# A four-layer graph network: neighbour rows of layers 2 and 3 summed by VectorE into a pair of sums in PSUM, in place of TensorE products with the identity

## The chip, the cores and the metric

The kernel runs on one core of a Trainium2 chip. The metric is the device time of one execution in microseconds (us), as the median of several runs. TensorE is PE (its weight loads PEld), VectorE is DVE, ScalarE is ACT, GpSimd is POOL, SyncE is SP.

## The reference

Four graph layers, each behind a layer norm, a ReLU and a residual, over 6250 nodes of 256 features and 106,250 edges (100,000 random ones and a loop per node). Layer 0 is attention with 8 heads of 32, layer 1 a gated recurrent update, layer 2 a relational layer with 8 edge types, layer 3 a graph attention with a batch norm. The two that the change touches, cut to their core:

```python
# layer 2: h = relu(layernorm(x))
hW = einsum('nd,rde->rne', h, weight)
m = segment_sum(hW[edge_type, src], dst)
x = x + h @ sl_w.T + sl_b + m / maximum(deg, 1)
...
# layer 3: loops added to the edges
xh = (x @ W).reshape(N, H, D)
e = leaky_relu(a_src[src] + a_dst[dst], 0.2)
alpha = softmax of e over the edges of each dst
out = segment_sum(xh[src] * alpha, dst) + bias
return batchnorm(out) + x
```

Both are sums over the neighbours of a node: plain in layer 2, weighted per head in layer 3. All values are float32.

## The kernel before

The nodes are sorted by the number of their edges and cut into 49 blocks of 128 (one node per partition). Every block has a number of slots, `CAPS`, one neighbour of each of its 128 nodes per slot: 39, 25, 24, 23, and so on down to 9, in all 822. A prefix builds these lists on the chip.

Each layer is a stage ("f0" to "f3") with a loop over the 49 blocks. A stage gathers the 822 slots with one indirect DMA each, issued by POOL: 128 rows of 1 KB, one to each partition (in layer 3 rows of 264 floats, the last 8 the heads' attention terms). `Slots.fill` takes a tile `v` for a chunk of up to 8 slots and issues its gathers (L1129). A `v` tile comes from a pool with a fixed number of buffers (8 in layer 2, 7 in layer 3); when all are in use POOL waits until the last reader of the oldest is done. Stages f0 and f1 have an order written by hand; in f2 and f3 the tile scheduler lays down the order of each engine's instructions from the loop. Every engine then runs its own list in order and waits on semaphores.

Layer 2 (stage f2), block by block: for every slot PE multiplies the slot's rows by the identity and adds up in PSUM tile `pa` (L1516; a float32 product is two passes). SP loads the block's x into `xb` (L1518). DVE makes xb = pa * (1/degree) + xb (L1519), then the layer norm on DVE and ACT (L514 to L523, ACT L523 the ReLU), transposes on PE (L531) copied by ACT (`ht`, L533), xb + h stored as x of layer 3 (L1523, L1524), the product with layer 3's weights (L540), its copy by ACT into `xa` (L1528), the attention terms on DVE (L1530, L1531) kept in `asd`, and the store of `xa` to DRAM (L1534). `xa` is what layer 3 gathers.

Layer 3 (stage f3), block by block: gathers into `v`; for each chunk, once it has landed, DVE adds attention terms into `s` (L1556); the own row's term (L1560), leaky ReLU (L1561), and in `weights_of` the softmax: mask (L1611), maximum (L1615), subtract (L1616), exp on ACT (L1617), the loop's factor (L1619), sum (L1621), reciprocal (L1622), and the weights into PSUM tile `ps_w` (L1624). SP loads the block's own rows `xh` (L1565). DVE multiplies xh by its weight (L1567) and PE puts it into PSUM tile `pm` (L1569); DVE multiplies each chunk in place by its weights (L1572), PE adds every slot to `pm` (L1574). DVE adds the bias into `o` (L1575), ACT squares it (L1584), PE adds o and its square over the nodes for the batch norm (L1586). In the program's order the L1556 of a later block stands among the work of earlier ones. After the last block come the norm, the residual and 49 scatters of rows to the output (L1123, POOL).

For scale: in f1, DVE already adds up slots, there with both operands in SBUF (L1386 to L1393).

Of the kernel before, what the change touches and what calls it, by code (L numbers as in the profile page):

```python
# [8 lines left out]
F32 = mybir.dt.float32  # L9
BF16 = mybir.dt.bfloat16  # L10
I32 = mybir.dt.int32
AF = mybir.ActivationFunctionType
# [5 lines left out]
P = 128  # L18
# [8 lines left out]
D = 256  # L27
H = 8
DH = 32
# [1118 lines left out]
class Fast(Kernel):  # L1148
# [13 lines left out]
    def ps(self, shape, kind):  # L1162
        return self.psum.tile(shape, F32, name="ps_" + kind, tag="ps_" + kind, bufs=self.bufs[kind])

    def constants(self):
        nc = self.nc
        self.ident = self.c([P, P], F32, "ident")
        make_identity(nc, self.ident)
        self.icol = self.c([P, 1], F32, "icol")
        nc.gpsimd.iota(self.icol, pattern=[[1, 1]], base=0, channel_multiplier=1,  # L1170
                       allow_small_or_imprecise_dtypes=True)
        self.ones = self.c([P, P], F32, "ones")
        nc.vector.memset(self.ones, 1.0)
        self.eps = self.c([P, 1], F32, "eps")
        nc.vector.memset(self.eps, EPS)
# [63 lines left out]
def sparse(ctx: ExitStack, tc: tile.TileContext, K, S, qv_d, h1_d, rel_d, xa_d, rows_d, wc_d, bc_d, b_ih, w_hh,  # L1239
           b_hh, w_rel, w_sl, b_sl, w_gat, att_src, att_dst, b_gat, gamma, beta, out):  # L1240

    nc = tc.nc
# [3 lines left out]
    with K.stage("f0", a=4, w=2, k=2), tc.tile_pool(name="f0", bufs=2) as pool:  # L1246
        heads = lambda x: x.rearrange("p (h d) -> p h d", h=H)
# [107 lines left out]
    rel_idx = K.c([P, NB, J], I32, "rel_idx")  # L1355
    with K.stage("f1", t=2, g=3, m=3), tc.tile_pool(name="f1w", bufs=1) as wp, tc.tile_pool(name="f1", bufs=2) as pool:
# [132 lines left out]
        with tc.manual_schedule(engines={nc.tensor.engine, nc.vector.engine, nc.scalar.engine}):  # L1489
            for k in range(NB + 4):  # L1490
                s, p, g, m, o = (f(order[k - d]) if 0 <= k - d < NB else nothing()
                                 for d, f in enumerate((sums, products, gates, messages, selves)))
# [8 lines left out]


    asd = ctx.enter_context(tc.tile_pool(name="asd", bufs=1)).tile([P, NB, 2, H], F32, name="asd", tag="asd")
    with K.stage("f2", t=2, m=4, a=2), tc.tile_pool(name="f2w", bufs=1) as wp, tc.tile_pool(name="f2", bufs=2) as pool:
        w = K.weights(wp, w_gat, "w_gat")
        att = wp.tile([P, 2, D], F32, name="att", tag="att")
        for k, vec in enumerate((att_src, att_dst)):
            nc.sync.dma_start(att[:, k, :], bass.AP(tensor=vec.tensor, offset=vec.offset,
                                                    ap=[[0, P], [1, D]]))
        for i in range(NB):  # L1510
            nd = CAPS[i]
            pa = K.ps([P, D], "a")
            for c, n in S.chunks(i, 8):
                v = S.fill(pool, "v", 8, rel_d, i, c, n, 8, D, rel_idx)
                for j in range(n):
                    nc.tensor.matmul(pa, K.ident, v[:, j, :], start=c + j == 0, stop=c + j == nd - 1)  # L1516
            xt = pool.tile([P, D], F32, name="xb", tag="xb")
            nc.sync.dma_start(xt, K.block(x2_d, i))  # L1518
            nc.vector.scalar_tensor_tensor(xt, pa, S.rcnt[:, i: i + 1], xt, op0=ALU.mult, op1=ALU.add)  # L1519
            h = K.norm(pool, xt)  # L1520
            ht = K.transposed(pool, h, "ht")

            nc.vector.tensor_add(xt, xt, h)  # L1523
            nc.sync.dma_start(K.block(x3_d, i), xt)  # L1524
            pm = K.ps([P, D], "m")
            K.product(pm, ht, w)
            xa = pool.tile([P, D + H], F32, name="xa", tag="xa")
            nc.scalar.activation(xa[:, :D], pm, AF.Copy)  # L1528
            tmp = pool.tile([P, 2, D], F32, name="tmp", tag="tmp")
            nc.vector.tensor_mul(tmp, att, xa[:, None, :D].to_broadcast([P, 2, D]))  # L1530
            nc.vector.tensor_reduce(asd[:, i], tmp.rearrange("p a (h d) -> p a h d", h=H), axis=AX.X,  # L1531
                                    op=ALU.add)
            nc.scalar.activation(xa[:, D:], asd[:, i, 0, :], AF.Copy)
            nc.sync.dma_start(K.block(xa_d, i), xa)  # L1534


    with K.stage("f3", m=2, a=2, w=2), tc.tile_pool(name="f3w", bufs=1) as wp, tc.tile_pool(name="f3", bufs=2) as pool:
        bias = K.row(wp, b_gat, D, "b_gat")
        gam = K.row(wp, gamma, D, "gamma")
        bet = K.row(wp, beta, D, "beta")  # L1540
        o = wp.tile([P, NB, D], F32, name="o", tag="o")

        twice = wp.tile([P, NB], F32, name="twice", tag="twice")
        nc.vector.tensor_scalar_add(twice, S.own, 1.0)
        x3 = wp.tile([P, NB, D], F32, name="x3", tag="x3")
        sums = [K.ps([P, D], "m") for _ in range(2)]
        first = wp.tile([P, D], F32, name="first", tag="first")
        for i in range(NB):
            n = P if i < NB - 1 else NLAST
            nd = CAPS[i]  # L1550
            nc.sync.dma_start(x3[:, i, :], K.block(x3_d, i))
            s = pool.tile([P, J + 1, H], F32, name="s", tag="s", bufs=3)
            held = []
            for c, m in S.chunks(i, 8):
                v = S.fill(pool, "v", 7, xa_d, i, c, m, 8, D + H, S.idx)
                nc.vector.tensor_add(s[:, c: c + m, :], v[:, :m, D:],  # L1556
                                     asd[:, i, 1, None, :].to_broadcast([P, m, H]))
                held.append((c, m, v))

            nc.vector.tensor_add(s[:, nd, :], asd[:, i, 0, :], asd[:, i, 1, :])  # L1560
            nc.vector.scalar_tensor_tensor(s[:, : nd + 1, :], s[:, : nd + 1, :], NEG_SLOPE,  # L1561
                                           s[:, : nd + 1, :], op0=ALU.mult, op1=ALU.max)
            w = weights_of(K, pool, s, nd, S.mneg[:, i, :nd], 1.0, twice=twice[:, i: i + 1])
            xh = pool.tile([P, D], F32, name="xh", tag="xh")
            nc.sync.dma_start(xh, K.block(xa_d, i)[:, :D])  # L1565
            xv = xh.rearrange("p (h d) -> p h d", h=H)
            nc.vector.tensor_mul(xv, xv, w[:, nd, :, None].to_broadcast([P, H, DH]))  # L1567
            pm = K.ps([P, D], "a")
            nc.tensor.matmul(pm, K.ident, xh, start=True, stop=False)  # L1569
            for c, m, v in held:  # L1570
                vv = v[:, :m, :D].rearrange("p j (h d) -> p j h d", h=H)
                nc.vector.tensor_mul(vv, vv, w[:, c: c + m, :, None].to_broadcast([P, m, H, DH]))  # L1572
                for j in range(m):
                    nc.tensor.matmul(pm, K.ident, v[:, j, :D], start=False, stop=c + j == nd - 1)  # L1574
            nc.vector.tensor_add(o[:, i, :], pm, bias)  # L1575
            if i == 0:

                pf = K.ps([P, D], "a")
                nc.tensor.matmul(pf, K.ones, o[:, 0, :], start=True, stop=True)
                nc.vector.tensor_scalar(first, pf, 1.0 / P, None, op0=ALU.mult)  # L1580
                nc.vector.tensor_sub(o[:, 0, :], o[:, 0, :], first)
                nc.vector.tensor_sub(bias, bias, first)
            sq = pool.tile([P, D], F32, name="sq", tag="sq")
            nc.scalar.activation(sq, o[:, i, :], AF.Square)  # L1584
            for p, x in zip(sums, (o[:n, i, :], sq[:n, :])):
                nc.tensor.matmul(p, K.ones[:n, :], x, start=i == 0, stop=i == NB - 1)  # L1586
        mean, shift, sc = (wp.tile([P, D], F32, name=x, tag=x) for x in ("mean", "shift", "sc"))
        nc.vector.tensor_scalar(mean, sums[0], 1.0 / N, None, op0=ALU.mult)
        nc.vector.tensor_mul(shift, mean, mean)
        nc.vector.scalar_tensor_tensor(sc, sums[1], 1.0 / N, shift, op0=ALU.mult, op1=ALU.subtract)  # L1590
        nc.vector.tensor_scalar_max(sc, sc, 0.0)
        nc.scalar.activation(sc, sc, AF.Sqrt, bias=K.eps)
        nc.vector.reciprocal(sc, sc)
        nc.vector.tensor_mul(sc, sc, gam)
        nc.vector.tensor_mul(mean, mean, sc)
        nc.vector.tensor_sub(shift, bet, mean)
        for b0, m in [(0, 1), (1, 2), (3, 3)] + [(b, min(4, NB - b)) for b in range(6, NB, 4)]:
            ob, xb = o[:, b0: b0 + m, :], x3[:, b0: b0 + m, :]
            nc.vector.tensor_mul(ob, ob, sc[:, None, :].to_broadcast([P, m, D]))
            nc.vector.tensor_add(xb, xb, shift[:, None, :].to_broadcast([P, m, D]))  # L1600
            nc.vector.tensor_add(xb, xb, ob)
            for i in range(b0, b0 + m):
                n = P if i < NB - 1 else NLAST
                S.scatter(out, S.node(i)[:n], x3[:n, i, :], "out")
# [211 lines left out]
```

## Time and profile before

| what | us |
|---|---|
| median of 3 runs | 4894.41 (4892.23 to 4895.73) |
| the profiled execution | 5607.33 |
| its span | 5605.5 |
| gathers of layer 0, first start to last | 368.0 to 1621.8 |
| layer 1 | 1679.0 to 2982.9 |
| layer 2 | 3060.2 to 4251.5 |
| layer 3 | 4287.7 to 5459.4 |
| scatters of the output | 5489.7 to 5589.0 |

The profile is of one execution, which took 713 us longer than the median of the runs; its mean granted TensorE clock is 0.706 of full. A group's row in the profile tells line, engine, operation and tiles, then busy time, mean duration in ns, and the engine's idle time ahead of it with what ended it ("issue": nothing that the profile shows; "remote": a signal whose sender it can't name). A timeline row has start, duration, engine, line and tiles.

POOL's idle time ahead of L1129, by what ended it, over the whole span: PE L1574 70.6 us (25 times), PE L1516 56.4 (26 times), "remote" 191.2 (48 times).

### The profile page before, as it was taken

The numbers are of one execution on the slowest core, as the hardware profiler recorded it, in microseconds if no ns is written. First come the engines' busy times: TensorE is split into PE (matmuls) and PEld (weight loads), VectorE is DVE, ScalarE is ACT, GpSimd is POOL, SyncE is SP. The second block draws the span as 40 slices with busy tenths as digits, with TensorE's granted clock in tenths as the row PEclk, the third lists the DMA queues.
The fourth block names the chain that finished last, engine by engine and source line by source line (L and its number), as shares of the span: only waits on it lengthen the run. The fifth ranks groups of instructions, "written<-read, shape, count | busy, mean of one in ns | idle before, by whom it ended". The sixth has DMA issues, their size and how long they took to land. (4 is left out here: it accounts for less than half of the span.)

```text
span 5605.5 us, 32468 instructions
## 1 busy us (share of the span) xinstructions
PE 2734.4 (49%) x8412; PEld 1806.8 (32%) x8413; DVE 2620.8 (47%) x5034; ACT 858.1 (15%) x1807; POOL 3448.3 (62%) x3546
## 2 busy tenths in 40 slices
PE   5654444444444766665445443433443544555551
PEld 2323323333332333332222232333332333333440
DVE  4437768776774776766665011111111333333343
ACT  2320111111221332322222000000011000000000
POOL 4326666666646665666663666666665666666666
PEclk7876666666666877877767576766776667766775
DMA  4466667676745544454442333333334333333331
GB/s 156 134 202 196 192 204 207 200 211 199 208 146 166 159 148 147 149 156 144 151 139 93 97 104 104 100 104 108 110 114 145 96 99 101 101 101 100 100 100 47
DMA packets 328275, 775.54 MB, mean 138 GB/s; under 512 B 87464, under 2 KB 172324, under 8 KB 321552
## 3 DMA queue, kind: packets, MB, share of 16 engines
q0 software_dynamic: 196864, 595.62, 37.3%
q1 hardware_dynamic: 117358, 163.66, 8.6%
q10 hardware_dynamic: 13858, 14.09, 0.8%
q8 instruction: 70, 1.15, 0.1%
q14 instruction: 125, 1.02, 0.1%
HBM read 637.90 MB, written 135.19 MB: 138 GB/s over the span
## 5 line engine op out<-in xcount | busy, mean ns | idle before, releaser
L1129 POOL DMA_INDIRECT v<-h,rec_in x822 | 848.6, 1032 | 454.3 <-issue 237.1
L1129 POOL DMA_INDIRECT v<-rel,rel_idx x822 | 789.5, 960 | 479.4 <-issue 234.5
L1129 POOL DMA_INDIRECT v<-xa,rec_in x822 | 783.6, 953 | 424.0 <-issue 265.7
L1129 POOL DMA_INDIRECT qv<-qv,rec_in x822 | 783.9, 954 | 412.2 <-issue 380.1
L1300 PE MATMUL ps_a<-qv,ident 128*128 128x256 f32 x1644 | 517.2, 471 | 251.7 <-issue 238.6
L1574 PE MATMUL ps_a<-v,ident 128*128 128x256 f32 x1644 | 473.7, 442 | 129.7 <-issue 122.7
L1300 PEld LDWEIGHTS ps_a<-qv,ident 128*128 128x128 f32 x1644 | 391.6, 242 | 385.0 <-issue 285.6
L1516 PE MATMUL ps_a<-v,ident 128*128 128x256 f32 x1644 | 463.4, 435 | 91.9 <-issue 75.0
L540 PE MATMUL ps_m<-w_rel,h2t 128*128 128x512 f32 x784 | 438.9, 723 | 35.1 <-ACT res L1466 19.0
L1574 PEld LDWEIGHTS ps_a<-v,ident 128*128 128x128 f32 x1644 | 372.8, 228 | 225.6 <-issue 151.2
L1516 PEld LDWEIGHTS ps_a<-v,ident 128*128 128x128 f32 x1644 | 357.5, 222 | 175.1 <-issue 94.9
L1262 DVE TENSOR_TENSOR tmp<-qv,ps_k 128x1280 f32<-128x1280 f32 (+4 forms) x183 | 247.1, 1350 | 215.1 <-DMA qv<-qv,rec_in 130.2
L1295 PE MATMUL ps_a<-row,ident 128*128 128x256 f32 x98 | 58.5, 698 | 486.0 <-issue 244.3
L1530 DVE TENSOR_TENSOR tmp<-att,xa 128x512 f32<-128x512 f32 x49 | 34.0, 693 | 557.2 <-ACT xa L1528 389.6
L540 PEld LDWEIGHTS ps_m<-w_rel,h2t 128*128 128x128 f32 x784 | 182.3, 240 | 260.0 <-issue 224.0
L1263 DVE TENSOR_REDUCE s<-tmp 128x40 f32<-128x1280 f32 (+4 forms) x183 | 247.2, 1351 | 10.0 <-DVE tmp L1262 2.0
L531 PE MATMUL ps_t<-ident,h 128*128 128x128 f32 x196 | 50.6, 347 | 388.1 <-ACT h L523 183.8
L1298 DVE TENSOR_TENSOR qv<-qv,ps_w 128x1280 f32<-128x1280 f32 (+4 forms) x183 | 235.0, 1345 | 0.0
L1519 DVE SCALAR_TENSOR_TENSOR xb<-ps_a,rcnt_in,xb 128x256 f32<-128x256 f32 x49 | 23.7, 484 | 448.4 <-remote 363.6
L1572 DVE TENSOR_TENSOR v<-v,ps_w 128x2048 f32<-128x2048 f32 (+7 forms) x124 | 233.0, 1914 | 0.0
L1409 PE MATMUL ps_t<-ident,total 128*128 128x128 f32 x98 | 31.2, 417 | 399.5 <-DVE total L1403 269.8
L540 PE MATMUL ps_m<-w_gat,ht 128*128 128x256 f32 x196 | 80.4, 552 | 290.5 <-ACT ht L533 191.2
(298 smaller groups left out, 4139.0 us busy)
## 6 DMA issues: line engine op xcount, KB each, us to landing
rel<-res SPq DMA_DIRECT2D x49, 1024.0 KB
rows<-mrow SPq DMA_DIRECT2D x49, 512.0 KB
fx<-xb SPq DMA_DIRECT2D x147, 128.0 KB
qv<-qv,rec_in POOLq DMA_INDIRECT x822
v<-h,rec_in POOLq DMA_INDIRECT x822
v<-rel,rel_idx POOLq DMA_INDIRECT x822
v<-xa,rec_in POOLq DMA_INDIRECT x822
qv<-mrow ACTq DMA_DIRECT2D x49, 256.0 KB
```

The lines of the kernel that those rows point to most:

```text
L531: nc.tensor.transpose(pt[:, k, :], x[:, k * P: (k + 1) * P], self.ident)
L540: self.nc.tensor.matmul(out, xt[:, k, :], w[:, k, :], start=start and k == 0, stop=stop and k == n - 1)
L1129: self.nc.gpsimd.indirect_dma_start(out=out, out_offset=None, in_=table, in_offset=bass.IndirectOffsetOnAxis(ap=idx, axis=0))
L1262: nc.vector.tensor_mul(tmp[:, :n, :], qv[:, :n, :D], pk[:, None, :].to_broadcast([P, n, D]))
L1263: nc.vector.tensor_reduce(s[:, c: c + n, :], tmp[:, :n, :].rearrange("p j (h d) -> p j h d", h=H), axis=AX.X, op=ALU.add)
L1295: nc.tensor.matmul(pm, K.ident, row[:, 2, :], start=True, stop=False)
L1298: nc.vector.tensor_mul(v, v, w[:, c: c + n, :, None].to_broadcast([P, n, H, DH]))
L1300: nc.tensor.matmul(pm, K.ident, qv[:, j, D: 2 * D], start=False, stop=c + j == nd - 1)
L1516: nc.tensor.matmul(pa, K.ident, v[:, j, :], start=c + j == 0, stop=c + j == nd - 1)
L1530: nc.vector.tensor_mul(tmp, att, xa[:, None, :D].to_broadcast([P, 2, D]))
L1572: nc.vector.tensor_mul(vv, vv, w[:, c: c + m, :, None].to_broadcast([P, m, H, DH]))
L1574: nc.tensor.matmul(pm, K.ident, v[:, j, :D], start=False, stop=c + j == nd - 1)
```

## The change

A new helper, `both`, ends a sum: ACT copies the second half of a [128, 2, 256] PSUM tile to SBUF, DVE adds it to the first half. Layer 2's `pa` and layer 3's `pm` become such pairs. In layer 2 ACT copies the first two slots into the pair, and DVE adds the others, two slots (512 elements) at a time, PSUM onto PSUM; the `v` tiles have 10 buffers in place of 8. In layer 3 DVE multiplies the own row straight into the pair's first half and slot 0 into its second; the other slots are multiplied in place as before and added two at a time; the 7 buffers stay. The PE products at L1516, L1569 and L1574 go. The number of PSUM tiles of each kind changes (f2: products 4 to 2, sums 2 to 4; f3: sums 2 to 4), and `sq` has 3 buffers.

Lines after the helper move down by 7, and further on by more: the first copy is L1525, layer 2's adds L1527, `both` L1168 (ACT) and L1169 (DVE), L1556 becomes L1568, L1572 and L1567 become L1579, layer 3's adds are L1592, L1575 becomes L1595.

```diff
@@ -1162,6 +1162,13 @@
     def ps(self, shape, kind):
         return self.psum.tile(shape, F32, name="ps_" + kind, tag="ps_" + kind, bufs=self.bufs[kind])
 
+    def both(self, pool, sums):
+
+        rest = pool.tile([P, D], F32, name="rest", tag="rest")
+        self.nc.scalar.activation(rest, sums[:, 1, :], AF.Copy)
+        self.nc.vector.tensor_add(sums[:, 0, :], sums[:, 0, :], rest)
+        return sums[:, 0, :]
+
     def constants(self):
         nc = self.nc
         self.ident = self.c([P, P], F32, "ident")
@@ -1501,7 +1508,7 @@
 
 
     asd = ctx.enter_context(tc.tile_pool(name="asd", bufs=1)).tile([P, NB, 2, H], F32, name="asd", tag="asd")
-    with K.stage("f2", t=2, m=4, a=2), tc.tile_pool(name="f2w", bufs=1) as wp, tc.tile_pool(name="f2", bufs=2) as pool:
+    with K.stage("f2", t=2, m=2, a=4), tc.tile_pool(name="f2w", bufs=1) as wp, tc.tile_pool(name="f2", bufs=2) as pool:
         w = K.weights(wp, w_gat, "w_gat")
         att = wp.tile([P, 2, D], F32, name="att", tag="att")
         for k, vec in enumerate((att_src, att_dst)):
@@ -1509,11 +1516,16 @@
                                                     ap=[[0, P], [1, D]]))
         for i in range(NB):
             nd = CAPS[i]
-            pa = K.ps([P, D], "a")
+            pa = K.ps([P, 2, D], "a")
             for c, n in S.chunks(i, 8):
-                v = S.fill(pool, "v", 8, rel_d, i, c, n, 8, D, rel_idx)
-                for j in range(n):
-                    nc.tensor.matmul(pa, K.ident, v[:, j, :], start=c + j == 0, stop=c + j == nd - 1)
+                v = S.fill(pool, "v", 10, rel_d, i, c, n, 8, D, rel_idx)
+                for k in range(0, n, 2):
+                    m = min(2, n - k)
+                    if c + k == 0:
+                        nc.scalar.activation(pa, v[:, :2, :], AF.Copy)
+                    else:
+                        nc.vector.tensor_add(pa[:, :m, :], pa[:, :m, :], v[:, k: k + m, :])
+            pa = K.both(pool, pa)
             xt = pool.tile([P, D], F32, name="xb", tag="xb")
             nc.sync.dma_start(xt, K.block(x2_d, i))
             nc.vector.scalar_tensor_tensor(xt, pa, S.rcnt[:, i: i + 1], xt, op0=ALU.mult, op1=ALU.add)
@@ -1534,7 +1546,7 @@
             nc.sync.dma_start(K.block(xa_d, i), xa)
 
 
-    with K.stage("f3", m=2, a=2, w=2), tc.tile_pool(name="f3w", bufs=1) as wp, tc.tile_pool(name="f3", bufs=2) as pool:
+    with K.stage("f3", m=2, a=4, w=2), tc.tile_pool(name="f3w", bufs=1) as wp, tc.tile_pool(name="f3", bufs=2) as pool:
         bias = K.row(wp, b_gat, D, "b_gat")
         gam = K.row(wp, gamma, D, "gamma")
         bet = K.row(wp, beta, D, "beta")
@@ -1563,15 +1575,23 @@
             w = weights_of(K, pool, s, nd, S.mneg[:, i, :nd], 1.0, twice=twice[:, i: i + 1])
             xh = pool.tile([P, D], F32, name="xh", tag="xh")
             nc.sync.dma_start(xh, K.block(xa_d, i)[:, :D])
-            xv = xh.rearrange("p (h d) -> p h d", h=H)
-            nc.vector.tensor_mul(xv, xv, w[:, nd, :, None].to_broadcast([P, H, DH]))
-            pm = K.ps([P, D], "a")
-            nc.tensor.matmul(pm, K.ident, xh, start=True, stop=False)
+            heads = lambda x: x.rearrange("p j (h d) -> p j h d", h=H)
+            times = lambda out, x, j0, j1: nc.vector.tensor_mul(
+                heads(out), heads(x), w[:, j0:j1, :, None].to_broadcast([P, j1 - j0, H, DH]))
+
+            pm = K.ps([P, 2, D], "a")
+            times(pm[:, 0:1, :], xh[:, None, :], nd, nd + 1)
             for c, m, v in held:
-                vv = v[:, :m, :D].rearrange("p j (h d) -> p j h d", h=H)
-                nc.vector.tensor_mul(vv, vv, w[:, c: c + m, :, None].to_broadcast([P, m, H, DH]))
-                for j in range(m):
-                    nc.tensor.matmul(pm, K.ident, v[:, j, :D], start=False, stop=c + j == nd - 1)
+                k = 0
+                if c == 0:
+                    times(pm[:, 1:2, :], v[:, :1, :D], 0, 1)
+                    k = 1
+                times(v[:, k:m, :D], v[:, k:m, :D], c + k, c + m)
+                while k < m:
+                    n2 = min(2, m - k)
+                    nc.vector.tensor_add(pm[:, :n2, :], pm[:, :n2, :], v[:, k: k + n2, :D])
+                    k += n2
+            pm = K.both(pool, pm)
             nc.vector.tensor_add(o[:, i, :], pm, bias)
             if i == 0:
 
@@ -1580,7 +1600,7 @@
                 nc.vector.tensor_scalar(first, pf, 1.0 / P, None, op0=ALU.mult)
                 nc.vector.tensor_sub(o[:, 0, :], o[:, 0, :], first)
                 nc.vector.tensor_sub(bias, bias, first)
-            sq = pool.tile([P, D], F32, name="sq", tag="sq")
+            sq = pool.tile([P, D], F32, name="sq", tag="sq", bufs=3)
             nc.scalar.activation(sq, o[:, i, :], AF.Square)
             for p, x in zip(sums, (o[:n, i, :], sq[:n, :])):
                 nc.tensor.matmul(p, K.ones[:n, :], x, start=i == 0, stop=i == NB - 1)
```

## The prediction

> **What bounds the kernel now.** I read the page's busy shares first, then its costliest groups, then the windows cut at the stages.
>
> ```profile
> PE 2734.4 (49%) x8412; PEld 1806.8 (32%) x8413; DVE 2620.8 (47%) x5034; ACT 858.1 (15%) x1807; POOL 3448.3 (62%) x3546
> ...
> L1129 POOL DMA_INDIRECT v<-rel,rel_idx x822 | 789.5, 960 | 479.4 <-issue 234.5
> L1129 POOL DMA_INDIRECT v<-xa,rec_in x822 | 783.6, 953 | 424.0 <-issue 265.7
> ...
> L1574 PE MATMUL ps_a<-v,ident 128*128 128x256 f32 x1644 | 473.7, 442 | 129.7 <-issue 122.7
> ...
> L1516 PE MATMUL ps_a<-v,ident 128*128 128x256 f32 x1644 | 463.4, 435 | 91.9 <-issue 75.0
> ```
>
> ```profile
> 3060.00:4255.00 1195.00, 526.46 (x1850) 401.18 (x1848) 146.32 (x360) 83.10 (x222) 789.46 (x822) 0.68 0.36 106
> 4255.00:5430.00 1175.00, 566.08 (x1898) 434.01 (x1898) 404.28 (x771) 41.89 (x113) 763.51 (x801) 0.69 0.38 104
> ```
>
> The columns of the windows are length, then PE, PEld, DVE, ACT, POOL, granted clock, DMA share, GB/s. In layers 2 and 3 POOL is the busiest engine by far. Its 0.30 us "issue" after each gather is part of the gather's price, so its pace is start to start. The timeline of layer 2 shows that:
>
> ```profile
> 3599.50 0.95 POOL L1129 DMA_INDIRECT v<-rel,rel_idx  x1 [0.31 <-issue]
> 3600.75 0.95 POOL L1129 DMA_INDIRECT v<-rel,rel_idx  x1 [0.30 <-issue]
> 3602.01 0.95 POOL L1129 DMA_INDIRECT v<-rel,rel_idx  x1 [0.31 <-issue]
> ...
> 3619.05 0.38 ACT L533 ACTIVATE ht<-ps_t 128x256 f32<-128x256 f32 x1 [27.56 <-remote]
> ...
> 3619.97 0.95 POOL L1129 DMA_INDIRECT v<-rel,rel_idx  x1 [5.70 <-remote]
> ```
>
> One gather takes 1.257 us. 822 of them are 1033 us; layer 2's gathers run from 3060.2 to 4251.5 (1191), layer 3's from 4287.7 to 5459.4 (1172). So 158 and 139 us are stalls, which look like PE's fault: POOL waits for a buffer that PE has not freed. The last two rows say otherwise. ACT at 3619.05 waits for transposes whose PE rows ended at 3592.2; for 27 us nothing that PE finished reached anyone, and then everything moved at once. I read that as a burden of the profiled execution. The check is a sum over POOL's path without such stalls: 366.7 (start of layer 0's gathers) + 3288 x 1.257 = 4133 + 49 row gathers 62 + layer 1's longer gathers 822 x (1.032-0.953) = 65 + the gaps between stages 54, 76 and 35 + 29 to the first scatter + 49 scatters 62 = 4883 us. The profiled execution took 5607.33, the median of the runs is 4894.41. The runs thus have about 11 us of POOL stalls left in four layers, where the profile has some 700. I forecast against the median: a removed PE wait is worth nothing much, a new wait counts in full.
>
> **Layer 2.** Gone are 1644 PE passes. They lie beside POOL: PE is busy 526 of 1195 us even in the profile, so their end is worth 0 to 11 us (that remainder); I take 0. New on DVE are 374 adds (L1527) and 49 in `both`, new on ACT 98 copies. No row has DVE with PSUM on both sides. The near rows, 512 elements wide:
>
> ```profile
> L1530 DVE TENSOR_TENSOR tmp<-att,xa 128x512 f32<-128x512 f32 x49 | 34.0, 693 | 557.2 <-ACT xa L1528 389.6 <-issue 167.5
> ...
> L1575 DVE TENSOR_TENSOR o<-ps_a,b_gat 128x256 f32<-128x256 f32 x43 | 18.2, 423 | 360.8 <-remote 216.4 <-PE ps_a L1574 136.3 <-issue 8.0
> ```
>
> L1428, 512 wide with one PSUM operand, takes 684 ns, L1530 wholly in SBUF 693: PSUM shows no surcharge. The Trainium skill speaks against that (Perfetto Trace Analysis, Optimizing Scalar/DVE Operations): DVE pays about 60 ns of access per instruction on SBUF and about 125 on PSUM. By the row an add is 0.69, 0.72 start to start in a chain; by the rule, with 65 ns more, 0.785, so 797 adds are 574 or 626 us. I take the row; the 52 us between them are DVE time, and reach POOL only where DVE is late. In layer 2 DVE goes to 146 + 374 x 0.72 + 49 x 0.43 = 436 us of 1033. In the changed program's order on DVE, the add that frees a chunk stands at least 47 gathers (59 us) from anything it must wait for, thanks to ten buffers. So layer 2 costs 0. ACT's copies (about 0.6 and 0.38 us, from L1528's 383 ns for 256 wide) add 48 us to 83, under the same cover; without it `both` would add 0.8 us to each block's chain, 39 us. That happens once: before layer 3 starts POOL waits for the last block's xa, whose sum now ends with adds, copy and `both` in place of two PE passes: +2 us.
>
> **Layer 3.** PE loses L1569 and L1574, worth 0 again (0 to 11, shared with layer 2). DVE gains 423 adds and 49 in `both`, about 326 us on 404: 730 of 1033. By block: one of 9 slots has about 10 to 11.4 us on DVE against 9 x 1.257 = 11.3 on POOL, one of 16 about 15.5 against 20.1. So DVE doesn't bound, on average. But it runs in order, and now it is the engine that frees chunks. This is DVE's order from one block of 19 slots in the changed program:
>
> ```
> 4783 L1568 TensorTensor s_17287<-v_17298,asd_13287 128x64 [waits DMASW4_49,DMASW5_49,DMASW3_49,DMASW6_49,DMASW2_49,DMASW7_49,DMASW1_49,DMASW0_49]
> 4784 L1592 TensorTensor ps_a_17262<-ps_a_17262,v_17222 128x512 [waits DVE_49]
> 4785 L1568 TensorTensor s_17287<-v_17308,asd_13287 128x24 [waits DMASW3_49,DMASW2_49,DMASW1_49]
> 4786 L1568 TensorTensor s_17353<-v_17354,asd_13287 128x64 [waits DMASW4_49,DMASW5_49,DMASW3_49,DMASW6_49,DMASW2_49,DMASW7_49,DMASW1_49,DMASW0_49]
> 4787 L1592 TensorTensor ps_a_17262<-ps_a_17262,v_17222 128x256 [waits DVE_49]
> ```
>
> Chunk v_17222 is block i's first, v_17354 is block i+2's first, and row 4787 is the last reader of v_17222. L1568 waits until all eight gathers of its chunk have landed. With seven buffers, three of block i, three of i+1 and the first of i+2 fill the pool; the next gather needs v_17222's buffer. So POOL, having issued the eighth gather of v_17354, must wait until that very gather has landed and DVE has done rows 4786 and 4787. Before, PE freed the chunk and didn't stand behind L1556, so the nearest such wait was 9 gathers off. What landing takes, from layer 3's timeline before:
>
> ```profile
> 4931.57 0.95 POOL L1129 DMA_INDIRECT v<-xa,rec_in  x1 [0.30 <-issue]
> ...
> 4934.49 0.23 DVE L1556 TENSOR_TENSOR s<-v,asd 128x64 f32<-128x64 f32 x1 [9.72 <-DMA v<-xa,rec_in]
> ```
>
> From the start of the last gather to DVE's start: 2.92 us (2.8 to 3.2 elsewhere). The skill's fit (DMA: Bandwidth & Descriptors, Anatomy of one DMA — SWDGE (gpsimd) path: 2.0 us plus bytes over 436 GB/s) gives 2.3 for 132 KB; the row decides, as it includes the issue. A place thus costs 2.92 + 0.23 (L1568) + 0.42 (add) + about 0.1 (signals) - 1.257 (the start that would have come anyway) = 2.4 us; by the rule 1.8. Walking the order with seven buffers, it occurs at 14 places: blocks 4 to 6 and 11 to 21, the ones with three chunks where the look-ahead stands so. At four of them another 0.7 us of add lies between. 10 x 2.4 + 4 x 3.2 = 37 us; by the rule 28. Bounds: 0 if the runs' landing is hidden, 60 if it takes 4.5 us as at layer 3's start (5.4 to 5.7 there).
>
> Block 0 (39 slots, five chunks). POOL wants its first chunk back at 4356.86 in the profile. DVE has the weights at 4350.5, and then, in the new order, own row and slot 0 (0.84), the multiplies of chunks 1 to 5 (2.0 + 3 x 2.28 + 2.0) and between them chunk 1's adds (3 x 0.72 + 0.42): 14.3 us, free at 4364.8, so 7.9 us late. Before, chunk 1 was free after its multiply and 16 PE passes of 0.24 us, about 4357.2, in the profile later only by the stall. So +7.5. After the last gather of layer 3, adds and `both` of the last two blocks replace PE work: +3.6 us before the final norm. The third sq buffer and the wider PSUM tiles cost 0.
>
> **Sum.** 0 + 2 + 37 + 7.5 + 3.6 = 50 us; 4894 + 50 = 4944. An add that is 0.1 us dearer brings some 8 us more, landing at 4.5 us 25 more, landing by the rule 9 less: own range 4915 to 4985.
>
> **Rivals.**
> Faster: the stalls are the kernel's, in the runs too, and other things in my sum of 4883 are shorter there. For: POOL's waits are named "PE ps_a". Then PE leaving the path takes, say, half of 297 us, 148 - 50 = 98 net: 4796. Against: the sum leaves only 11 us. It decides in this rival's favour if more than 60 us of PE waits exist in the runs. Chance 0.17, with small gains as likely as large.
> Same: DVE is ahead of my walk, or the waits fall into stalls that are there anyway, or the adds' waits are as before; or the change doesn't do what it says, as PE was never in the way and DVE isn't either. 4894. Chance 0.08.
> Slower by more, at DVE against POOL: in layer 1, where DVE sums slots, gathers take 1032 ns and not 953. If adds in layers 2 and 3 do this, 1644 x 0.079 = 130 us: 5074 with the waits. For it: the one stage with such sums. Against: layer 1's adds read two SBUF operands, the new ones one. Chance 0.05. The main case is itself on the slower side: 0.70.
>
> **Numbers.** Faster 0.17, within 0.2% (10 us, about what a measurement can tell from no change) 0.08, slower 0.75. Range 4875 to 5000: main case with its bounds, same case, and the smallest gains; left out are larger gains (0.14) and the 130 us.
>
> **What will show it.** Right: 14 waits of POOL in layer 3 on DVE L1592, each 2 to 3.5 us, always with L1568 just before; block 0's of 7 to 8; none in layer 2; adds at 0.69 us; gathers at 1.257. In the profiled execution the PE-flush stalls of layers 2 and 3 should shrink, so its own time may fall while the runs rise. Wrong: runs below 4885, or waits by DVE in layer 2, or L1592 above 0.85 us.

## The result, and the profile after

The changed kernel takes 4941.68 us (median of 4 runs, 4939.28 to 4944.01) against 4894.61 of the kernel before (4892.23 to 4895.73): 47.1 us more, a ratio of 1.0097 (95% interval 1.0079 to 1.0114). The forecast was 4944. In the profile of before, and in the jobs (sets of executions measured together) of ten of the twelve kernels below, every execution was stretched: it took some 600 to 700 us more, the kernel before's too, so such numbers are compared only with the kernel before in the same job.

The profiled execution of the changed kernel, with a span of 4938.8 us, is one of the four runs above, so it shows what the runs do. Its page, the rows that answer to those of before:

```profile
PE 1776.5 (36%) x5027; PEld 1050.7 (21%) x5027; DVE 3077.0 (62%) x5978; ACT 918.5 (19%) x1954; POOL 3469.6 (70%) x3546
...
L1129 POOL DMA_INDIRECT v<-rel,rel_idx x822 | 792.0, 963 | 307.7 <-issue 229.4
L1129 POOL DMA_INDIRECT v<-xa,rec_in x822 | 786.6, 957 | 313.8 <-issue 254.5
L1129 POOL DMA_INDIRECT qv<-qv,rec_in x822 | 786.8, 957 | 250.6 <-issue 201.9
L1527 DVE TENSOR_TENSOR ps_a<-ps_a,v 128x512 f32<-128x512 f32 (+1 forms) x374 | 254.7, 681 | 605.6 <-DMA v<-rel,rel_idx 592.9
```

The windows of layers 2 and 3 (columns as before):

```profile
2650.00:3711.00 1061.00, 135.51 (x296) 71.72 (x296) 395.94 (x824) 132.40 (x344) 791.99 (x822) 0.50 0.41 121
3711.00:4795.00 1084.00, 96.62 (x186) 54.41 (x186) 618.85 (x1273) 52.70 (x141) 786.65 (x822) 0.50 0.41 115
```

PE's busy time in the two layers is down to 136 and 97 us, DVE has its work, and POOL is as busy as it was (792 and 787 us). Layer 2's gathers start from 2651.77 to 3692.89 us, 1041 us: 822 at POOL's pace, 1.261 us from start to start in the median, without one longer wait. Layer 3's, from 3711.95 to 4793.37, take 1081. What POOL waited for (total, times, longest; a wait of 0.3 is the ordinary step between gathers):

```profile
POOL v L1129 <- DVE s L1573: 31.5, 11, 3.0
...
POOL v L1129 <- DVE ps_a L1527: 14.0, 46, 0.3
...
POOL v L1129 <- DVE s L1631: 11.0, 3, 3.9
POOL v L1129 <- DVE s L1568: 7.7, 1, 7.7
...
POOL v L1129 <- DVE ps_a L1592: 2.4, 8, 0.3
```

Layer 2's adds (L1527) hold POOL at no place. Layer 3 has 11 + 3 + 1 waits, 45.7 us of the 47.1 when each is counted without its 0.30 us step. Counting layer 3's gathers from zero, the fourteen stand before gathers 163, 184, 205, 303, 322, 340, 358, 376, 394, 412, 429, 446, 463 and 480: the second chunk of blocks 6 to 8 and 13 to 23, two blocks after those that the prediction names, as it said. The single one is at gather 55, block 0's buffer. One of the fourteen in the timeline, before gather 184:

```profile
3952.95 0.96 POOL L1129 DMA_INDIRECT v<-xa,rec_in  x1 [0.30 <-issue]
3956.10 0.22 DVE L1568 TENSOR_TENSOR s<-v,asd 128x64 f32<-128x64 f32 x1 [7.29 <-DMA v<-xa,rec_in]
3956.24 0.42 DVE L1592 TENSOR_TENSOR ps_a<-ps_a,v 128x256 f32<-128x256 f32 x1
3956.58 0.33 DVE L1573 SCALAR_TENSOR_TENSOR s<-s 128x176 f32<-128x176 f32 x1
3956.82 0.69 DVE L1592 TENSOR_TENSOR ps_a<-ps_a,v 128x512 f32<-128x512 f32 x1
3956.94 0.95 POOL L1129 DMA_INDIRECT v<-xa,rec_in  x1 [3.03 <-DVE s L1573]
```

DVE sits idle for 7.29 us until the gather of 3952.95 has landed; only then comes the last add on the old chunk (3956.24), and POOL goes on 0.28 us after that add ends. The releaser named, L1573, is the row that ended nearest to POOL's start; what POOL needed is the add ahead of it, the last reader of the buffer. So read the rows before the restart, not the name alone.

### The profile page after: what moved, and what is told of

It is laid out like the page before. It is cut to its first block, busy times and chain, and to the rows that moved or that the text cites. A ratio compares the mean times of both kernels' runs of the same rounds, so it can differ in the third digit from the quotient of the medians.

```text
span 4938.8 us, 27151 instructions
## 1 busy us (share of the span) xinstructions
PE 1776.5 (36%) x5027; PEld 1050.7 (21%) x5027; DVE 3077.0 (62%) x5978; ACT 918.5 (19%) x1954; POOL 3469.6 (70%) x3546
## 5 line engine op out<-in xcount | busy, mean ns | idle before, releaser
L1527 DVE TENSOR_TENSOR ps_a<-ps_a,v 128x512 f32<-128x512 f32 (+1 forms) x374 | 254.7, 681 | 605.6 <-DMA v<-rel,rel_idx 592.9
L1307 PE MATMUL ps_a<-qv,ident 128*128 128x256 f32 x1644 | 456.4, 446 | 9.1 <-DVE qv L1305 9.0
L1307 PEld LDWEIGHTS ps_a<-qv,ident 128*128 128x128 f32 x1644 | 372.0, 230 | 108.8 <-DVE qv L1305 44.1
L1606 PE MATMUL ps_m<-o,ones 128*128 128x256 f32 (+1 forms) x98 | 59.8, 714 | 898.7 <-DVE o L1595 896.0
L1568 DVE TENSOR_TENSOR s<-v,asd 128x64 f32<-128x64 f32 (+7 forms) x124 | 26.3, 212 | 464.3 <-DMA v<-xa,rec_in 447.6
L1393 DVE TENSOR_TENSOR v<-v 128x512 f32<-128x512 f32 (+2 forms) x211 | 187.5, 889 | 183.9 <-DMA v<-h,rec_in 158.0
L1592 DVE TENSOR_TENSOR ps_a<-ps_a,v 128x512 f32<-128x512 f32 (+1 forms) x423 | 277.1, 655 | 0.4
L531 PEld LDWEIGHTS ps_t<-ident,h 128*128 128x128 f32 x196 | 26.2, 187 | 1086.4 <-ACT h L523 800.0
L1606 PEld LDWEIGHTS ps_m<-o,ones 128*128 128x128 f32 (+1 forms) x98 | 24.5, 311 | 934.0 <-DVE o L1595 930.6
L1579 DVE TENSOR_TENSOR v<-v,ps_w 128x1792 f32<-128x1792 f32 (+7 forms) x124 | 220.4, 1811 | 0.0
L1486 DVE SCALAR_TENSOR_TENSOR xb<-res,ownr,xb 128x256 f32<-128x256 f32 x392 | 190.7, 487 | 10.9
```

Source lines behind the costliest of these rows:

```text
L531: nc.tensor.transpose(pt[:, k, :], x[:, k * P: (k + 1) * P], self.ident)
L1307: nc.tensor.matmul(pm, K.ident, qv[:, j, D: 2 * D], start=False, stop=c + j == nd - 1)
L1393: nc.vector.tensor_add(v[:, :k, :D], v[:, :k, :D], v[:, m - k: m, :D])
L1486: nc.vector.scalar_tensor_tensor(xt, res[:, r, :], S.ownr[:, i, r: r + 1], xt, op0=ALU.mult, op1=ALU.add)
L1527: nc.vector.tensor_add(pa[:, :m, :], pa[:, :m, :], v[:, k: k + m, :])
L1579: times = lambda out, x, j0, j1: nc.vector.tensor_mul(heads(out), heads(x), w[:, j0:j1, :, None].to_broadcast([P, j1 - j0, H, DH]))
```

## The experiments

The expectations weigh these readings of the 47 us. Theory A: POOL waits for chunk buffers in layer 3, because of where DVE's adds stand in its order. Theory B: the adds cost by their number or price, wherever they stand. Theory C: layer 2 gains by PE's absence, and layer 3 loses more than the whole shows. Theory D (in e3): in source order DVE has too little room. Edits are cut to their core; a minus stands for the changed kernel, in e6 for the kernel before.

**Layer 2 alone** (e1, and e10 in another job): the changed kernel with all lines of layer 3's stage as before, at their core

```diff
-                    nc.vector.tensor_add(pm[:, :n2, :], pm[:, :n2, :], v[:, k: k + n2, :D])
+                    nc.tensor.matmul(pm, K.ident, v[:, j, :D], start=False, stop=c + j == nd - 1)
```

> Layer 2 as in the change (DVE adds, ten buffers), layer 3 as before. Theory A (POOL's pace sets the time, the loss sits in layer 3's chunk buffers): no POOL wait in layer 2, about 2 us more at the step from layer 2 to 3, so 4896 to 4898 us against 4894.6, ratio 1.0005. Theory B (DVE adds in PSUM cost wherever they stand): 374 of the 797 adds, so 47 x 374/797 = 22 us, 4917. Theory C (layer 2 gains by PE's absence and layer 3 loses more than the whole shows): below 4885.

> Layer 2 as in the change, layer 3 as before, in the hope of a job that runs the kernel before at about 4895 us. Theory A: no POOL wait in layers 2 and 3, the time within 5 us of before's (4890 to 4899), as PE's sums were never what POOL waited for. Theory C (PE's sums did hold POOL up somewhere, and layer 3's waits hid that in the whole): below 4885.

Measured: 5492.07 against 5533.10 in the first job, ratio 0.9926 (0.9896 to 0.9957); 5546.36 against 5581.08 in the second, 0.9940 (0.9921 to 0.9959). Both jobs were stretched, so the absolute times expected do not apply. There, layer 2 gains: its gathers took 1124.0 and 1126.6 us, where those of the kernel before took 1169.9 in the profile of another stretched job (e12) and 1191.3 on the page of before. This is what theory C expected, though only in these executions: in the result's own profile layer 2's gathers are at POOL's pace, and the kernel before has little room for such a gain in its runs, as the account below says. The row of layer 2 in e10's windows:

```profile
3052.00:4180.00 1128.00, 124.26 (x270) 65.86 (x270) 382.32 (x777) 122.72 (x319) 855.68 (x822) 0.50 0.39 112
```

POOL is busy 856 us with the same 822 gathers that took 792 in the result's profile; its own gathers are drawn out.

**Layer 3 alone** (e2): the changed kernel with all lines of layer 2's stage as before.

```diff
-                v = S.fill(pool, "v", 10, rel_d, i, c, n, 8, D, rel_idx)
+                v = S.fill(pool, "v", 8, rel_d, i, c, n, 8, D, rel_idx)
...
-                        nc.vector.tensor_add(pa[:, :m, :], pa[:, :m, :], v[:, k: k + m, :])
+                    nc.tensor.matmul(pa, K.ident, v[:, j, :], start=c + j == 0, stop=c + j == nd - 1)
```

> Layer 3 as in the change, layer 2 as before. Theory A: the same 14 waits in layer 3, about 40 us, and block 0's, so 4894.6 + 45 = 4940 us (4935 to 4945), ratio 1.009. Theory B: 423 of 797 adds, 25 us, 4920. Theory C: above 4950.

Measured: 5541.00 against 5533.10, ratio 1.0021 (1.0006 to 1.0037): slower, by some 12 us at the ratio and not 45. In a stretched execution POOL stands still for some 130 to 150 us in each of layers 2 and 3 anyway; that a new wait falls partly into that is likely, not shown. The sign fits A; the size tells nothing apart.

**Layer 3's DVE in source order** (e3, e7, e9; e5 with layer 2 as before). Same instructions on DVE, same seven buffers; only the order is fixed:

```diff
-        for i in range(NB):
+        with tc.manual_schedule(engines={nc.vector.engine}):
+            for i in range(NB):
```

> The changed kernel, with layer 3's DVE instructions held in the order of the source: a block's multiplies and adds all stand before the next block's first s<-v. Same instructions, same seven buffers. Theory A: the add that frees a chunk no longer stands behind the wait for the chunk two blocks on, so the 14 waits and block 0's go: 4941.7 - 45 = 4897 us (4892 to 4902). Theory B (the adds themselves, their number or price in PSUM, are the cost): 4940, no change. Theory D (DVE has too little room once its work of one block and the next no longer overlap): new POOL waits on DVE in the blocks of 9 to 12 slots, 4910 or more.

> The changed kernel with layer 3's DVE instructions in the order of the source, once more, in the hope of a job [...](the kernel before at about 4895 us). Theory A (in-order waits of the adds against seven buffers are the loss): no POOL wait over 1 us in layer 3, its gathers 1036 us from first to last and not 1081, time 4897 us (4892 to 4902). Theory B (number or price of the adds): 4935 or more.

> The changed kernel with layer 3's DVE in source order, timed against the kernel before. One look gave 4886.7 against 4892.4. Where the kernel before takes about 4895: theory A, 0.998 to 0.9995 of it (the waits are gone, and the time from the last gather to the first scatter fell from 29.6 to 23.1 us, since no block's work is left over when the last one lands): 4886 to 4892 us. If that one look was luck: within 0.1% of before.

> Layer 2 as before (PE sums), layer 3 as in the change but with DVE's instructions in the order of the source. Where the kernel before takes about 4895 us: theory A (the loss is DVE's order against seven buffers) gives no POOL wait in layer 3 and 4893 to 4897 us; theory B (the adds themselves) 4920 or more. Where the kernel before takes about 5530 us, engines starve for reasons that this edit doesn't touch, layer 3's gathers stay at 1165 to 1180 us from first to last, and the time stays within 15 us of before's.

The decisive one is e7, in a job where the kernel before took 4892.41: 4886.70 us, 55.0 less than the changed kernel's median in the result and 5.7 less than the kernel before. That is one execution each; the four executions of either kernel in the result lie within 5 us. Its layer 3, and what POOL waited for there:

```profile
3709.00:4748.00 1039.00, 98.69 (x190) 55.52 (x190) 714.45 (x1290) 53.48 (x143) 786.47 (x822) 0.50 0.43 120
```

```profile
POOL v L1129 <- DVE ps_a L1593: 7.6, 25, 0.3
```

The adds are all there (DVE busy 714 us, more than in the changed kernel), and no wait is over 0.3 us; the gathers start from 3710.13 to 4745.77, 1035.6 us and not 1081.4. Theories B and D are out: neither the number of the adds nor their price in PSUM costs time here, only where they stand. From the last gather to the first scatter it takes 23.1 us, the changed kernel 29.6: in e7's trace no work of the block before is left over at the end. So of the 54 us between the two spans 45.8 lie in layer 3's gathers and 6.5 behind them. In the stretched jobs the same kernel made 5527.99 against 5533.10 (e3, 0.9992, 0.9974 to 1.0011) and 5562.91 against 5581.08 (e9, 0.9966, 0.9956 to 0.9976): not told apart in e3, faster in e9. But layer 2 alone gains more in the same jobs (e1, e10): against it, source order in layer 3 is 36 and 17 us slower. e5 agrees: 5564.20 against 5540.07, one execution each, outside the 15 us expected. Against e6 in its job, layer 3's gathers take 1178.6 us for 1163.4, and from the last of them to the first scatter it is 45.3 for 30.6. A likely reason is that DVE waits for its own signals in such executions (last section), and source order leaves it nothing else to do meanwhile; that is not tested.

**Six buffers in layer 3** (e8, in e7's job), the scheduler's order as it comes:

```diff
-                v = S.fill(pool, "v", 7, xa_d, i, c, m, 8, D + H, S.idx)
+                v = S.fill(pool, "v", 6, xa_d, i, c, m, 8, D + H, S.idx)
```

> The changed kernel with six chunk buffers in layer 3 in place of seven; the scheduler's order as it comes. Walking that order, a gather directly behind the one it must see landed occurs at 17 places in blocks of three and two chunks (2.3 us each by landing 2.9), a shorter one once, and block 0 waits some 16 us for its first chunk. Theory A: layer 3's stalls go from 46 to 61 us, time 4941.7 + 15 = 4957 us (4950 to 4965). Theory B: no change, 4942.

Measured: 4953.11 us against 4892.41, one execution each, 60.7 more (the seven buffers: 47.1 more). POOL's waits:

```profile
POOL v L1129 <- DVE s L1573: 38.3, 14, 3.0
...
POOL v L1129 <- DVE ps_a L1592: 22.8, 13, 17.8
...
POOL v L1129 <- DVE s L1572: 8.7, 3, 3.4
```

In layer 3 they sum to 60.6 us without the 0.30 steps, 17.5 of it block 0's: the time lost goes with the waits (60.7 and 60.6 us here, 47.1 and 45.7 with seven buffers), as theory A has it. Theory B expected 4942.

**Eight buffers of seven slots** (e4, and e11), the same memory:

```diff
-            for c, m in S.chunks(i, 8):
-                v = S.fill(pool, "v", 7, xa_d, i, c, m, 8, D + H, S.idx)
+            for c, m in S.chunks(i, 7):
+                v = S.fill(pool, "v", 8, xa_d, i, c, m, 7, D + H, S.idx)
```

> The changed kernel with layer 3's chunks of up to seven slots and eight buffers (the same memory as seven of eight slots); the scheduler's order as it comes. Theory A: one buffer more lies between a chunk and its reuse, so the wait is for gathers at least seven back and mostly hidden; some 5 us of waits remain, in block 0: 4941.7 - 37 = 4905 us (4898 to 4912). Theory B: 4940 or a little more, since there are more and smaller multiplies and adds.

> The changed kernel with layer 3's chunks of up to seven slots and eight buffers, once more, the scheduler's order as it comes. Walking that order, only block 0's wait of some 5 us is left. Theory A: 4941.7 - 41 = 4901 us (4896 to 4908). Theory B: 4940 or more. In a job that runs the kernel before at 5530 us nothing is told apart.

Measured: 5509.49 against 5533.10 (0.9950, 0.9935 to 0.9966), and 5548.92 against 5581.08 (0.9947, 0.9928 to 0.9965), both in stretched jobs. That is 17 us above layer 2 alone in the first job (e1) and 3 in the second (e10); e2 put layer 3's cost at some 12. So the buffers' share can't be read, and this way of taking the waits away stays untried where they count.

**Ten buffers in the kernel before** (e6), and **the kernel before once more** (e12), unedited, for its profile.

```diff
-                v = S.fill(pool, "v", 8, rel_d, i, c, n, 8, D, rel_idx)
+                v = S.fill(pool, "v", 10, rel_d, i, c, n, 8, D, rel_idx)
```

> The kernel before with ten chunk buffers in layer 2, nothing else of the change. Where the kernel before takes about 4895 us: theory A says there was no wait for a buffer in layer 2, so no change (4893 to 4897). Where it takes about 5530 us, layer 2 has PE signals that come in one flush once POOL stops; two more buffers only put the stop off by 16 gathers, so layer 2 stays at 1175 to 1190 us and the time within 10 us of before's; if the buffers were what helped layer 2, it falls to about 1125 and the time by 40 to 50 us.

> The kernel before, unedited, for its profile. If the job [...](about 4893 us): theory A says layers 2 and 3 show next to no POOL wait on PE, their gathers taking 1034 to 1041 us from first to last; theory C says 50 us or more of such waits in the two layers. If the job takes some 5540 us, it shows what the page of before shows, PE waits of 130 to 150 us a layer, and tells nothing apart.

Measured: 5541.47 against 5540.07, and 5518.88 against 5510.68, one execution each. Buffers alone do nothing there: e6's layer 2 took 1169.3 us, e12's 1169.9. So what helps layer 2 in the stretched jobs is that its sums leave PE, alone or together with the buffers. There is no trace of the kernel before that is not stretched.

## Why the prediction was right

**The bound.** POOL's pace sets layers 2 and 3: shown for DVE sums by e7, where both layers run at it, and for the kernel before only by sums. The 4883 came out close to the median partly by luck. The profile after gives: 330.3 before layer 0's gathers (I had 366.7); the four layers 1096.6, 1109.3, 1042.4 and, without its waits, 1037.0, each with the last gather's own step; gaps of 58.5, 57.3 and 17.8 (54, 76 and 35); 28.3 to the first scatter (29); scatters to the end of the span 115.9 (62: the first alone lasts 38.97). Together 4893, which is the span less layer 3's waits, so this splits the time and proves nothing by itself. My terms from the stretched profile were 68 us too long ahead of the gathers and in the gaps; the gathers were 25 too short, and for the scatters I had left out the long first one and the time behind the last, 54. Most of that cancels, so the "about 11 us" of stalls left was not as sharp as it looked.

**PE's waits are a burden of stretched executions.** The cleanest sign is in code that the change leaves alone: layers 0 and 1 have POOL waits over 0.5 us of 162 and 204 us on the page of before, and 0.3 and 0 in the profile after. That they cost little in the runs of the kernel before follows from two comparisons. e7, whose trace has no POOL wait over half a us at a gather of any layer, is only 5.7 us faster than the kernel before. And the changed kernel without its waits would take 4893 and the 2 us that an execution takes more than its span (4940.81 and 4938.8 for the profiled one), 4895 against 4894.6. Both take it that the gaps between the stages are alike in the two kernels. It was not seen in a trace of the kernel before itself.

**Layer 2 costs 0**: no wait, as said. **The price of an add**, by form:

```profile
L1592 DVE TENSOR_TENSOR ps_a<-ps_a,v 128x512 f32<-128x512 f32 x350 | 245.3, 701 | 0.3
L1527 DVE TENSOR_TENSOR ps_a<-ps_a,v 128x512 f32<-128x512 f32 x350 | 244.4, 698 | 594.5 <-DMA v<-rel,rel_idx 582.2 <-ACT ps_a L1525 7.5 <-ACT ht L533 4.7
```

0.70 us with PSUM on both sides: the row chosen (0.69) was right. The dearer price, 0.785 start to start, estimated with the Trainium skill's access times (Perfetto Trace Analysis, Optimizing Scalar/DVE Operations), is not seen; in e7 four in a chain take 2.90 us, with 0.73 from one start to the next:

```profile
3945.32 2.90 DVE L1593 TENSOR_TENSOR ps_a<-ps_a,v 128x512 f32<-128x512 f32 x4
```

**The fourteen waits**: 37 us forecast, 38.3 measured without the steps, at the gathers foreseen and by the mechanism foreseen. Eleven take 2.40 to 2.73, three 3.18 to 3.57 (four had been foreseen). In the place shown, landing took 3.15 us, the add started 0.14 after L1568 did and took 0.42, and POOL needed 0.28: 3.99 - 1.26 = 2.73. The estimate with landing by the Trainium skill's fit (DMA: Bandwidth & Descriptors, Anatomy of one DMA — SWDGE (gpsimd) path) was 28 in all: too low; the row's 2.92 us was the better guide.

**Block 0**: 7.5 forecast, 7.4 measured, by the path foreseen: the adds of its first chunk stand among the multiplies of its later ones, and POOL goes on when the last of them ends.

```profile
3788.01 0.43 DVE L1592 TENSOR_TENSOR ps_a<-ps_a,v 128x256 f32<-128x256 f32 x1
3788.34 0.22 DVE L1568 TENSOR_TENSOR s<-v,asd 128x64 f32<-128x64 f32 x1
3788.71 0.95 POOL L1129 DMA_INDIRECT v<-xa,rec_in  x1 [7.73 <-DVE s L1568]
```

**The steps at the ends** were too dear: 2 + 3.6 forecast, and 47.1 - 45.7 = 1.4 is all that is left for both. That the sum, 50, still came so close to 47.1 is due to the waits, which make up 45.7 of it.

**The rivals.** Faster: excluded for the runs of the result; in the stretched jobs layer 2's part does gain 0.6 to 0.7%, so this rival had a real mechanism in executions like the one on the page of before. DVE against POOL: gathers of layers 3 and 2 went from 953 and 960 to 957 and 963 ns, and those of layer 0, which has no new adds, from 954 to 957; no sign of the 79 ns that it needed. Layer 0's row before:

```profile
L1129 POOL DMA_INDIRECT qv<-qv,rec_in x822 | 783.9, 954 | 412.2 <-issue 380.1
```

## What to carry to other kernels

When an engine that runs in order takes over the last read of a buffer, look at what its instruction list has ahead of that read. A wait there for the chunk that was asked for last costs most of a landing each time (2.4 to 3.6 us here, fourteen times), however idle the engine is. An order that finishes one block before it looks at the next took these waits away (e7), though it was no gain in stretched executions; one buffer fewer made them longer and more (e8); more buffers are untried where it counts. And sum the path from the profile's steady pace before trusting its waits: an execution far above the median of the runs can have waits in every stage that the runs do not have.

## What the runs showed that was not expected

The same kernel took 4886.70 us (e7) and 5562.91 (e9) in two jobs. The trace of e7 holds 76,848 recorded signal updates of semaphores, that of e9 18,994; the profile of before 21,084, of after 76,970. This parts all the traces: the three that are not stretched have some 77,000, the eleven stretched ones 18,700 to 22,100. In e3's trace, between 4484.4 and 4494.9 us, DVE's instructions that wait for one another start 0.7 to 1.4 us apart though they take 0.2 to 0.5. Whether the recording causes this, or another thing holds up both the signals and their records, no run here tells; the stretched jobs also ran on other chips than e7's.

DVE was busy 619 us in layer 3, not the 730 of the forecast. Where an add alternates with a small instruction of another block, that one starts 0.60 us after the add, before the add's end, and two adds are 0.75 us apart with the small one between them, where in a chain of adds alone they are 0.73 apart:

```profile
3947.31 0.70 DVE L1592 TENSOR_TENSOR ps_a<-ps_a,v 128x512 f32<-128x512 f32 x1
3947.91 0.22 DVE L1568 TENSOR_TENSOR s<-v,asd 128x40 f32<-128x40 f32 x1
3948.06 0.69 DVE L1592 TENSOR_TENSOR ps_a<-ps_a,v 128x512 f32<-128x512 f32 x1
```

So the order that costs POOL its waits saves DVE 96 us against e7's 714.
